# A two-layer graph transformer on one core: the first four blocks of each layer as single tiles

## The chip, the cores and the metric

The kernel runs on one core of a Trainium2 chip. A core has five engines that run their own instruction streams and meet at semaphores: TensorE (PE) for matrix products, VectorE (DVE) and ScalarE (ACT) for element-wise work, GpSimd (POOL), which here mostly starts indirect DMAs, and SyncE (SP), which starts plain ones. Matrix products land in PSUM, everything else lives in SBUF. The metric is the device time of one execution in microseconds, as a median over runs.

## The reference, cut to what matters

There are 2708 tokens with 512 features, and a sparse symmetric adjacency (each row has a few entries beside the diagonal). Two layers with weights of their own do the same thing:

```python
mask = adj.astype(jnp.float32) + jnp.eye(n, dtype=jnp.float32)
q = (h @ Wq.T + bq).reshape(n, N_HEADS, D_K)      # 8 heads of 64
...
scores = jnp.einsum('nhd,mhd->hnm', q, k) / jnp.sqrt(jnp.float32(D_K))
scores = jnp.where(mask[None, :, :] == 0, jnp.float32(-1000000000.0), scores)
attn = jax.nn.softmax(scores, axis=-1)
ctx = jnp.einsum('hnm,mhd->nhd', attn, v).reshape(n, D_MODEL)
h1 = _layer_norm(h + ctx @ Wo.T + bo, ln1_g, ln1_b)
ff = jax.nn.relu(h1 @ W1.T + b1) @ W2.T + b2       # 2048 hidden
h2 = _layer_norm(h1 + ff, ln2_g, ln2_b)
```

Everything is computed in float32.

## The kernel before, in words

**Attention by lists.** The kernel turns the adjacency into lists of neighbours, at most 22 per token, sorts the tokens by the length of their list, and works on 22 tiles of 128 tokens (the last has 20). `CAPS` gives each tile's number of slots: tile 0 has 22, tile 20 has 5. For a slot, POOL gathers one row of keys and values (4 KB) per token. Slots go in chunks of two (`SLOTS`): tile 20 has chunks 20c0, 20c1 and 20c2, the last with one slot. `attend` (from L1436) is a generator; each `next` on it emits one step: the products with the query and their reduction for one chunk (`weights`, L1041 and L1047 on DVE), exp, scaling and summing for the chunk before (`weigh`, L1060 and L1067 on ACT, L1073 and L1080 on DVE), the sums of a tile two steps after its last chunk, and its division by the softmax sum three steps after (`divided`, L1111 on ACT, into `cx`). The step yields its cost, 1 for a chunk of two. After tile 19 and at the end three empty steps of cost 0.2 let these later parts run.

**How attention is woven into the rest.** `advance(more)` adds `more` to a credit and takes steps while the credit is above zero and fewer than two finished contexts wait in `got`. `through(k)` takes steps until block k's contexts are finished. So the code decides the order of the instructions; on PE, ACT and SP it is the order of execution (`manual_schedule`), on POOL it is so until block 0 of layer 0 is done. DVE's stream, and POOL's later, come out of a planner that starts whatever it deems ready first.

**Staging.** In layer 0, keys and values of all tiles are projected beside the building of the lists (`first`), then all queries (`first_queries`), with attention starting beside them. Then the tiles go through the feed-forward in `blocks`: eleven pairs, (20, 19), (18, 17), (7, 9) and so on. For the first block, projection and first normalisation (`attended`) are emitted within the query loop, at its step t = 19, after `through(0)`. For a later block they are emitted while the block before it is in its feed-forward: contexts are transposed at step f = 10 (11 in block 0 of layer 0), projected at the next step, and the normalised rows transposed after step 15 into `hT`, which has one buffer.

**One block's feed-forward** (`feed_forward`) has 16 steps. A step makes 128 of the 2048 hidden features, `pf` (L1351, four products over the block's 256 tokens, in one of three PSUM buffers), puts it through relu (`ft`, L1359, ACT), and three steps later (`LAG`) adds its share to the output sums (L1324), one PSUM accumulator per tile, `a0` and `a1`, with one buffer each. The last three shares come after step 15, tile by tile. DVE reads the accumulators (L1375) and normalises into z. A float32 product shows as two matmul records in the trace: a step of a pair has eight records of `pf` and four of `a`.

**What else runs in it.** In layer 0 each block's z is transposed at steps 5 to 8 of the next block and projected to keys and values of layer 1, which POOL scatters (`keys_values`, `behind`). In layer 1, queries of tiles from `order[16]` on are made late: `blocks[k + AHEAD]` with `AHEAD = 8`, so two per block in blocks 0 to 2, from transposed rows that SP loads. Block 0 of layer 0 also loads the last three pieces of W1 and W2, and layer 1's Wk and Wv, through ACT's queue. The credit per step is `PACE` (0.62 in layer 0, 0.72 in layer 1), and 1.1 up to step 10 and 0.4 after it in block 0 of both layers.

Of the kernel before, what the change touches and what calls it, by code (L numbers as in the profile page):

```python
# [18 lines left out]
P = 128  # L19
# [23 lines left out]
AHEAD = 8  # L43
# [6 lines left out]
PACE = (0.62, 0.72)  # L50
# [422 lines left out]
def by_edges(ctx: ExitStack, tc: tile.TileContext, x, xT, adj, layers, out, good):  # L473
# [125 lines left out]
    def size(g):  # L599
        return min(P, N - g * P)  # L600
# [302 lines left out]
    def first_queries(bq, wq, counts, ranked, listed, pa, tokens, meanwhile):  # L903

        nonlocal at
        made = []

        def written():
            t, qs = made.pop(0)
            if t + 2 < NT:  # L910
                out = q_d[0][t * P : (t + 2) * P, :].rearrange("(two p) c -> p two c", p=P)
                nc.sync.dma_start(out=out, in_=qs)
                return
            for i in range(2):
                r = size(t + i)
                nc.sync.dma_start(out=q_d[0][(t + i) * P : (t + i) * P + r, :], in_=qs[:r, i])

        for t in range(NT):
            r = size(t)
            if t % 2 == 0 and made:  # L920
                written()
            q = project(tokens(t, 1), r, wq, "q", other=t % 2 > 0)
            if t == 0:
                ranked(*counts)
                xrs = [own_rows(g) for g in order[:3]]
            if t % 2 == 0:
                qs = wts.tile([P, 2, DM], F32, tag=f"w2_{5 + t // 2 % 3}", name="qs")
                made.append((t, qs))
            nc.vector.scalar_tensor_tensor(
                qs[:r, t % 2], q[:r], DK**-0.5, bq[:r], ALU.mult, ALU.add  # L930
            )
            plus_rest(qs[:r, t % 2], q, r, DK**-0.5)
            if t == OWN - 1:
                listed(True)
                pa.__exit__(None, None, None)
                at = ctx.enter_context(tc.tile_pool(name="at", bufs=2))
                for g in order[:3]:
                    own[g] = at.tile([P, DM], F32, tag="q", name="q", bufs=QB)
                to = dict(own)
                next(ahead)  # L940
            if t == OWN:
                zTs = [turned_own(g, xr) for g, xr in zip(order, xrs)]
                for g, zT in zip(blocks[0], zTs):
                    own_query(g, zT, to[g], bq, wq)
                    advance(0.5)
            if t == OWN + 1:
                listed(False)
                xr = own_rows(order[3])
            if t == OWN + 4:
                own_query(order[2], zTs[2], to[order[2]], bq, wq)  # L950
                zT = turned_own(order[3], xr)
            meanwhile(t)
            if t == NT - 1:
                g = order[3]
                own[g] = at.tile([P, DM], F32, tag="q", name="q", bufs=QB)
                own_query(g, zT, own[g], bq, wq)
        while made:
            written()
        all_made.append(True)
# [469 lines left out]
    now = Layer(0, layers[0])  # L1429


    blocks = [(20, 19), (18, 17), (7, 9), (6, 10), (5, 11), (0, 16)]
    blocks += [(1, 15), (2, 14), (3, 13), (4, 12), (NT - 1, 8)]
    NB = len(blocks)
    order = [g for block in blocks for g in block]

    def attend(n, got):

        peak = small.tile([P, NT], F32, tag="peak", name="peak", bufs=1)
        nc.vector.memset(peak, 0.0)  # L1440
        loaded = loads(n)
        steps = []
        for g in order:
            cuts = chunks_of(g)
            steps += [(g, s0, c, i, i + 1 == len(cuts)) for i, (_, s0, c) in enumerate(cuts)]
            if g == order[1]:
                steps += [None] * 3
        steps += [None] * 3
        kv = next(loaded)
        yield 0.0  # L1450
        q = asked(n, order[0])
        done = [None] * 3
        for k, step in enumerate(steps):
            if step:
                g, s0, c, i, last = step
                if i == 0:
                    while q is None:
                        q = asked(n, g)
                        if q is None:
                            yield None  # L1460
                    t, q = Tile(g, q), None
                if k > 0:
                    kv = next(loaded)
                t.weights(kv, s0, c)
                if i > 0 and q is None and g != order[-1]:
                    q = asked(n, order[order.index(g) + 1])
                done.append((t, kv, s0, c, last))
            else:
                done.append(None)
            t3, t2, t1 = done[-4:-1]  # L1470
            if t1:
                t1[0].weigh(*t1[1:4])
            if t2 and t2[-1]:
                t2[0].sums(peak)
            if t3 and t3[-1]:
                got[t3[0].g] = t3[0].divided()
            yield c / SLOTS if step else 0.2
        nc.vector.tensor_reduce(flags[:, 4 + n : 5 + n], peak, AX.X, ALU.max)
        nc.vector.tensor_scalar(
            flags[:, 4 + n : 5 + n], flags[:, 4 + n : 5 + n], SAFE, None, ALU.is_le  # L1480
        )
# [3 lines left out]
    def advance(more):  # L1485

        nonlocal credit
        credit = min(credit + more, 1.5)
        while credit > 0 and len(got) < CXB - 1:
            cost = next(ahead, None)  # L1490
            if cost is None:
                break
            credit -= cost
# [44 lines left out]
    behind, pool = None, []  # L1538
    for n in range(NL):
        last = n == NL - 1  # L1540
        nxt = None if last else Layer(n + 1, layers[n + 1])
        if n > 0:
            streamed = now.queries(order[8 : 2 * AHEAD])
            got = {}
            ahead = attend(n, got)
            with tc.manual_schedule(engines={mybir.EngineType.DVE}):
                for _ in range(2):
                    now.query(*pool.pop(0))
                next(ahead)
                next(streamed)  # L1550
                while pool:
                    advance(0.4)
                    now.query(*pool.pop(0))
                for i in range(2 * AHEAD - 10):
                    advance(0.4)
                    next(streamed)
                through(0)
                early[n] = now.attended(blocks[0], got)
                next(early[n])
                for _ in blocks[0]:  # L1560
                    next(early[n])
                finish(streamed)
            now.load_w2(NFC // 2 - 1)
# [6 lines left out]
        for k, block in enumerate(blocks):  # L1570
            more = k + 1 < NB
            asking = iter(())
            if n > 0 and k + AHEAD < NB:
                asking = now.queries(blocks[k + AHEAD])
            for f, zs in enumerate(now.feed_forward(block, hs, hT)):
                if f == NFC:
                    break
                if f in (5, 6, 7, 8) and behind:
                    next(behind)
                if more and f == 10 + (k + n == 0):  # L1580
                    through(k + 1)
                    projecting = now.attended(blocks[k + 1], got)
                    next(projecting)
                if more and f == 11 + (k + n == 0):
                    for hs_next in projecting:
                        advance(0.5 if k else 0.0)
                advance(PACE[n] if k else 1.1 if f < 11 else 0.4)
                if f in (0, 3, 7, 9):
                    next(asking, None)
                if more and f == NFC - 1:  # L1590
# [5 lines left out]
                if n > 0 and (k, f) == (0, 2):  # L1596
                    now.load_second(1, temp)
                if not last:
                    if (k, f) == (0, 10):
                        now.load_next()  # L1600
                        now.kv = [matrix(nxt.w, "Wk", "wk", nc.scalar)]
                    if (k, f) == (0, 13):
                        now.kv.append(matrix(nxt.w, "Wv", "wv", nc.scalar))
                    if (k, f) == (NB - 1, 0):
                        finish(ahead)
                        places.clear()
                        now.wq = matrix(nxt.w, "Wq", "wq")
                    if f == 1 and k in (1, 3):
                        i, name, scale = (1, "bk", 1.0) if k == 1 else (0, "bq", DK**-0.5)
                        turning = turned_row(now.cols[i], name, scale)  # L1610
                        rows_of = now if k == 1 else nxt
                        setattr(rows_of, name, next(turning))
                    if f == 3 and k in (1, 3):
                        finish(turning)
# [19 lines left out]
        else:  # L1634
# [8 lines left out]
            now = nxt  # L1643
# [63 lines left out]
```

## Time and profile before

Three runs took 1942.04 us in the median (1936.44 to 1943.61).

| What | us |
|---|---|
| the profiled execution | 1946.15 |
| its span, first to last instruction | 1944.3 |
| PE busy | 1858.4 |
| DVE busy | 1321.0 |
| ACT busy | 934.7 |
| POOL busy | 809.3 |
| PE idle before transposes of contexts, waiting for ACT (4 times) | 25.5 |
| PE idle before transposes of h, waiting for DVE (4 times) | 10.1 |

The mean granted PE clock is 0.981 of full speed. A line of the timeline gives the start and the length of a run of like instructions in us, the engine, the line of the kernel, the operation, its output and inputs by the program's names, shapes and count, and in brackets the idle time of the engine before it with what ended it. Matmuls overlap in the records, so a run's throughput is read from one start to the next. In the page's slices each digit is the busy share of a fortieth of the span in tenths.

### The profile page before, as it was taken

The numbers are of one execution on the slowest core, as the hardware profiler recorded it, in microseconds if no ns is written. First come the engines' busy times: TensorE is split into PE (matmuls) and PEld (weight loads), VectorE is DVE, ScalarE is ACT, GpSimd is POOL, SyncE is SP. The second block draws the span as 40 slices with busy tenths as digits, with TensorE's granted clock in tenths as the row PEclk, the third lists the DMA queues.
The fourth block names the chain that finished last, engine by engine and source line by source line (L and its number), as shares of the span: only waits on it lengthen the run. The fifth ranks groups of instructions, "written<-read, shape, count | busy, mean of one in ns | idle before, by whom it ended". The sixth has DMA issues, their size and how long they took to land. (4 is left out here: it accounts for less than half of the span.)

```text
span 1944.3 us, 20898 instructions
## 1 busy us (share of the span) xinstructions
PE 1858.4 (96%) x6162; PEld 1096.7 (56%) x6162; DVE 1321.0 (68%) x2172; ACT 934.7 (48%) x3219; POOL 809.3 (42%) x710
## 2 busy tenths in 40 slices
PE   9998968999999999999999997999999999999996
PEld 4443435556656556665665553566666666666663
DVE  5885467768759687695841237696987998877421
ACT  4660236445546655574451113555475767654510
POOL 3113526535536555364410124344555775546101
PEclk9999979999999999999999998999999999999998
DMA  9998848555646656554401478656665766643000
GB/s 322 355 314 299 275 136 302 172 179 184 205 138 201 217 188 197 177 183 154 146 17 65 136 246 325 202 197 204 203 222 168 251 222 220 209 155 125 17 6 14
DMA packets 131486, 366.92 MB, mean 189 GB/s; under 512 B 16668, under 2 KB 37004, under 8 KB 128654
## 3 DMA queue, kind: packets, MB, share of 16 engines
q0 software_dynamic: 69120, 246.35, 38.0%
q1 hardware_dynamic: 53332, 99.66, 14.8%
q10 hardware_dynamic: 8910, 19.48, 2.6%
q8 instruction: 50, 0.82, 0.2%
q14 instruction: 74, 0.61, 0.1%
HBM read 314.62 MB, written 50.83 MB: 188 GB/s over the span
## 5 line engine op out<-in xcount | busy, mean ns | idle before, releaser
L1004 POOL DMA_INDIRECT kv<-kv_d,idx x420 | 547.0, 1302 | 452.2 <-DVE acc L1080 273.5
L1351 PE MATMUL pf<-hT,w 128*128 128x256 f32 (+1 forms) x2816 | 637.2, 373 | 7.2 <-ACT ft L1359 5.2
L1324 PE MATMUL a<-w,ft 128*128 128x512 f32 x1344 | 632.2, 596 | 5.3 <-ACT ft L1359 4.4
L1351 PEld LDWEIGHTS pf<-hT,w 128*128 128x128 f32 x2816 | 521.2, 191 | 186.6 <-issue 106.5
L1359 ACT ACTIVATE ft<-pf,b 128x256 f32<-128x256 f32 (+1 forms) x352 | 160.3, 460 | 458.5 <-PE pf L1351 458.3
L1041 DVE TENSOR_TENSOR kv<-kv,q 128x1024 f32<-128x1024 f32 (+3 forms) x222 | 254.2, 1157 | 169.2 <-DMA kv<-kv_d,idx 131.1
L1324 PEld LDWEIGHTS a<-w,ft 128*128 128x128 f32 x1344 | 253.2, 191 | 198.6 <-issue 171.6
L1067 ACT ACTIVATE kv<-kv,p 128x64 f32<-128x64 f32 x1232 | 311.0, 335 | 5.0
L1047 DVE TENSOR_REDUCE sc<-kv 128x16 f32<-128x1024 f32 (+3 forms) x222 | 253.8, 1153 | 1.5
L1080 DVE TENSOR_TENSOR acc<-acc,kv 128x1024 f32<-128x1024 f32 (+2 forms) x178 | 204.0, 1146 | 18.9 <-ACT kv L1067 17.0
L1156 POOL TENSOR_TENSOR rd<-va,mhalf 128x1 f32<-128x1 f32 (+1 forms) x88 | 90.4, 1028 | 274.6 <-DVE va L1154 273.7
L576 PE MATMUL o<-wo,cT 128*128 128x512 f32 x336 | 151.1, 602 | 0.5 <-ACT cT L1171 0.5
L1073 DVE TENSOR_TENSOR kv<-kv,p 128x512 f32<-128x512 f32 (+1 forms) x178 | 121.4, 682 | 34.6 <-ACT p L1060 34.6
L1060 ACT ACTIVATE p<-sc,minus 128x8 f32<-128x8 f32 x420 | 102.8, 294 | 69.2 <-DVE sc L1047 62.1
L1111 ACT ACTIVATE cx<-acc,su 128x64 f32<-128x64 f32 (+1 forms) x352 | 88.5, 334 | 74.7 <-DVE su L1103 57.6
L576 PEld LDWEIGHTS o<-wo,cT 128*128 128x128 f32 x336 | 64.5, 193 | 83.2 <-issue 72.9
L681 ACT ACTIVATE code<-aj 128x2708 bf16<-128x2708 int32 (+1 forms) x22 | 73.3, 3332 | 49.2 <-POOL aj L677 49.0
L684 DVE MAX8 tops<-code 128x8 f32<-128x247 f32 (+2 forms) x242 | 83.1, 401 | 19.3 <-ACT code L681 19.3
L1160 DVE SCALAR_TENSOR_TENSOR h<-h,rd,ln_b 128x512 f32<-128x512 f32 (+1 forms) x88 | 65.6, 747 | 40.6 <-POOL rd L1156 40.6
L1067 ACT ACTIVATE acc<-kv,p 128x64 f32<-128x64 f32 (+1 forms) x352 | 88.8, 334 | 1.4
L1410 ACT COPY kvs<-v 128x512 f32<-128x512 f32 (+1 forms) x22 | 12.9, 586 | 158.9 <-PE v L576 138.5
L1375 DVE TENSOR_TENSOR h<-a,h 128x512 f32<-128x512 f32 (+1 forms) x44 | 29.9, 679 | 85.2 <-PE a L1339 48.8
(154 smaller groups left out, 1560.2 us busy)
## 6 DMA issues: line engine op xcount, KB each, us to landing
aj<-in_adj SPq DMA_DIRECT2D x21, 1354.0 KB, 8.4
kv_d<-kvs ACTq DMA_DIRECT2D x21, 512.0 KB, 7.4
w<-in_W SPq DMA_DIRECT2D x20, 512.0 KB, 6.5
xg<-in_xT SPq DMA_DIRECT2D x19, 512.0 KB, 8.6
kv<-kv_d,idx POOLq DMA_INDIRECT x420, 5.8
w<-in_W ACTq DMA_DIRECT2D x12, 512.0 KB, 7.2
q_d<-qs SPq DMA_DIRECT2D x22, 256.0 KB, 3.4
zT_d<-zT SPq DMA_DIRECT2D x22, 256.0 KB, 4.3
```

The costliest lines, as they stand in the source:

```text
L576: nc.tensor.matmul(o[:r], xs(c), wm[:, c, :], start=(c == 0), stop=(c == NC - 1))
L1004: nc.gpsimd.indirect_dma_start(out=to, out_offset=None, in_=table[:, :], in_offset=bass.IndirectOffsetOnAxis(ap=s, axis=0), bounds_check=N ...
L1041: nc.vector.tensor_tensor(kv[:r, :c, :DM], kv[:r, :c, :DM], self.q[:r].unsqueeze(1).to_broadcast([r, c, DM]), ALU.mult,)
L1047: nc.vector.tensor_reduce(self.sc[:r, s0 : s0 + c, :], kv[:r, :c, :DM].rearrange("p s (h d) -> p s h d", d=DK), AX.X, ALU.add,)
L1060: nc.scalar.activation(p[:r, s, :], self.sc[:r, s, :], AF.Exp, bias=minus[:r, g, s : s + 1])
L1067: nc.scalar.activation(to[:, i, hd], kv[:r, i, DM + h * DK : DM + (h + 1) * DK], AF.Copy, scale=p[:r, s0 + i, h : h + 1],)
L1073: nc.vector.tensor_tensor(to[:, 0, :].rearrange("p (h d) -> p h d", d=DK), kv[:r, 0, DM:].rearrange("p (h d) -> p h d", d=DK), p[:r, s0, : ...
L1080: nc.vector.tensor_tensor(self.acc[:r, :c, :], self.acc[:r, :c, :], kv[:r, :c, DM:], ALU.add)
L1156: nc.gpsimd.tensor_tensor(rd[:r], va[:r], mhalf[:r], ALU.pow)
L1324: nc.tensor.matmul(a[:r], fts[f][:, c0 : c0 + r], self.w2[f // 2][:, f % 2, :], start=(f == 0), stop=(f == NFC - 1),)
L1351: nc.tensor.matmul(pf[:, :w], self.w1[f // 2][:, c, f % 2 * P : f % 2 * P + P], hT[:, c, :w], start=(c == 0), stop=(c == NC - 1),)
L1359: nc.scalar.activation(ft[:, :w], pf[:, :w], AF.Relu, bias=self.b1[:, f : f + 1])
```

## The change

Tiles 20, 19, 18 and 17 become blocks of one tile each; the other nine blocks stay as they are, so a layer has thirteen blocks where it had eleven. What depends on the width of a block follows:

- `through(0)` and the projection of block 0 concern tile 20 alone; the three empty steps of attention after tile 19 are left out.
- A single tile's block transposes the next block's contexts at step 8 and projects them at step 9; for pairs these are steps 10 and 11 everywhere.
- A single tile's block advances attention by 0.45 a step, and by nothing beside the projection; pairs keep `PACE`, scaled by their tokens over 256 (1 for a full pair).
- Late queries of layer 1 are taken in order, as many as the block has tiles.
- Loads for layer 1 (`load_next`, Wk, Wv) move from steps 10 and 13 of block 0 to steps 6 and 9.

```diff
-                for g, zT in zip(blocks[0], zTs):
+                for g, zT in zip(order[:2], zTs):
...
-    blocks = [(20, 19), (18, 17), (7, 9), (6, 10), (5, 11), (0, 16)]
+    blocks = [(20,), (19,), (18,), (17,), (7, 9), (6, 10), (5, 11), (0, 16)]
...
-            if g == order[1]:
-                steps += [None] * 3
...
+            late = order[2 * AHEAD :]
...
-            if n > 0 and k + AHEAD < NB:
-                asking = now.queries(blocks[k + AHEAD])
+            wide = sum(size(g) for g in block) / (2 * P)
+            if n > 0 and late:
+                asking = now.queries(late[: len(block)])
+                late = late[len(block) :]
...
-                    next(behind)
-                if more and f == 10 + (k + n == 0):
+                    next(behind, None)
+                turn = 10 - 2 * (len(block) == 1)
+                if more and f == turn:
...
-                if more and f == 11 + (k + n == 0):
+                if more and f == turn + 1:
                     for hs_next in projecting:
-                        advance(0.5 if k else 0.0)
-                advance(PACE[n] if k else 1.1 if f < 11 else 0.4)
+                        advance(0.5 if len(block) > 1 else 0.0)
+                advance(PACE[n] * wide if len(block) > 1 else 0.45)
...
-                    if (k, f) == (0, 10):
+                    if (k, f) == (0, 6):
...
-                    if (k, f) == (0, 13):
+                    if (k, f) == (0, 9):
```

## The prediction

> **What bounds the kernel now.** I read the page's busy times first, then its slices, then the timeline of TensorE (PE) where the slices drop. PE is the bound: it is busy 96% of the span, VectorE (DVE) 68%, ScalarE (ACT) 48%.
>
> ```profile
> PE 1858.4 (96%) x6162; PEld 1096.7 (56%) x6162; DVE 1321.0 (68%) x2172; ACT 934.7 (48%) x3219; POOL 809.3 (42%) x710
> ...
> PE   9998968999999999999999997999999999999996
> ...
> PEclk9999979999999999999999998999999999999998
> ```
>
> Each digit is 48.6 us. PE drops in slice 6 (243 to 292 us) and slice 25 (1215 to 1264 us), and the granted clock drops with it: these are the entries into the feed-forward (FF) of the two layers, which the change touches. The timeline shows what is waited for there. First layer 0, columns: start, length, engine and line, operation, idle time before it and its releaser.
>
> ```profile
> 248.34 0.60 PE L1166 MATMUL tp<-ident,cx 128*128 128x128 f32 x4
> 263.15 1.91 PE L1166 MATMUL tp<-ident,cx 128*128 128x128 f32 x4 [14.21 <-ACT cx L1111]
> ...
> 285.24 1.11 PE L1166 MATMUL tp<-ident,h 128*128 128x128 f32 x4 [3.66 <-DVE h L1160]
> 286.81 9.03 PE L1351 MATMUL pf<-hT,w 128*128 128x256 f32 x32 [0.46 <-ACT hT L1171]
> ```
>
> Tile 20's context is transposed at 248.34; PE then sits 14.21 us for tile 19's, since both belong to block 0. Layer 1 repeats it:
>
> ```profile
> 1203.84 0.60 PE L1166 MATMUL tp<-ident,cx 128*128 128x128 f32 x4
> 1211.87 1.91 PE L1166 MATMUL tp<-ident,cx 128*128 128x128 f32 x4 [7.43 <-ACT cx L1111]
> ...
> 1232.91 7.17 PE L1351 MATMUL pf<-hT,w 128*128 128x256 f32 x32 [1.05 <-ACT hT L1171]
> ```
>
> Undisturbed work, for prices: a pair's FF step, and 128-column matmuls with a fresh weight load each.
>
> ```profile
> 601.05 1.04 PE L1166 MATMUL tp<-ident,h 128*128 128x128 f32 x8
> 601.93 5.32 PE L1324 MATMUL a<-w,ft 128*128 128x512 f32 x12
> ...
> 615.70 1.89 PE L1351 MATMUL pf<-hT,w 128*128 128x256 f32 x8
> 617.43 1.88 PE L1324 MATMUL a<-w,ft 128*128 128x512 f32 x4
> 619.15 1.89 PE L1351 MATMUL pf<-hT,w 128*128 128x256 f32 x8
> ```
>
> Start to start counts here, since lengths overlap. A pair's step is 619.15 - 615.70 = 3.45 us; eight 128-column matmul records take 601.93 - 601.05 = 0.88 us, 0.11 each; the 512-column ones 1.72 / 4 = 0.43.
>
> **Two rules of the Trainium skill.** "TensorE: Matmul & The Clock Gate", section on LDWEIGHTS, prices a weight load by its columns, 128 / 1.2 = 107 ns, so a matmul over 128 columns cannot run faster than its weights arrive. The trace agrees (0.11 us), and I use 0.11: the halved matmul costs just over half of the 256-column one (1.73 / 8 = 0.216), no cliff. Part 1 of the same page says that the clock halves after about 3.4 us of idleness. Here the v matmuls at 403.00, after only 2.05 us idle, took 5.40 us against 3.60 at 390.48, so shorter gaps cost too; the forecast goes by the trace.
>
> **The change, part by part.**
>
> *Matmul shape.* A single's step is 8 x 0.11 + 2 x 0.43 = 1.746 us (0.111 and 0.429 before rounding), 27.9 us for 16 steps; two singles cost 55.9 where a pair costs 16 x 3.45 = 55.1. Four singles stand for two pairs in each layer: +1.4 us a layer.
>
> *Entry of layer 0.* `through(0)` now needs tile 20 alone. But the three empty steps after tile 19 are gone, so the credits of the query loop (0.5 + 0.5 + 5 x 1.0 + 0.6) now also put 18c0 and 18c1 (tile 18's first two chunks) ahead of block 0's projection in program order on ACT and POOL, where in before they came behind it. On POOL, tile 20's row gather (246.68 in before) then stands behind the gather of 17c1, which waits for the buffer of 18c0: the DMA let DVE start 18c0 at 253.19; product and reduction take 2.5, exp and copies 2.5, so the buffer is free near 259.5. Two gathers of 1.3 and the row gather end near 264; landing takes 5 (5.8 median): h of tile 20 can be added at about 269, its normalisation takes 5.5 (275.4 to 280.9 in before), and DVE owes up to 2 us of other work: 276. Transpose and copy 1.6: FF starts near 278, not 286.8. PE then still owes tile 19's projection and transposes.
>
> *Blocks 0 to 3 of layer 0.* Before: 286.81 to 449.55 for blocks 0 and 1, 162.7 us. Their work at full rate is 110.3 (steps) + 4 projections of 3.43 + 10 transposes of 0.44 + 2 key-value tiles of 6.87 + one turned row 0.9 = 143.1; 19.6 us are idle time (5.2 for ACT in block 0's steps, 3.14, 0.85, 2.05) and half clock. After: 111.7 + 5 x 3.43 + 13 x 0.44 + 3 x 6.87 + 1.8 = 157, ending at 435 plus new stalls. Before reaches equal work at 449.55 + 7.3 (keys of tile 18) + 0.9 = 457.8. Gain 22.8 us, less the stalls.
>
> *Entry of layer 1.* Tile 20's cx was done at 1196.6, so projection follows its transpose at once: 1204.3 + 1.3 (copy) + 3.43 = 1209; two queries to 1216, under which the normalisation (3.9 us after the projection's end in before) hides; FF near 1217.8, not 1232.9. Owed: one projection and two transposes, 4.3. Gain 10.8, less 1.4 for shape.
>
> *New stalls.* PE's slack halves while DVE and ACT work per tile stays.
> - Accumulator `a0` (one buffer, L1324). In a pair, the first tile's sum is taken up by DVE 4.4 us (typical; 1.6 to 7.2) after its last matmul, while PE has 2.6 us of the other tile and 6.9 of the next block's first four groups. In a single, PE is back in `a0` after 4 x 0.888 = 3.55. The read ends at 4.4 + 0.7 = 5.1: 1.6 us, at three boundaries per layer: 9.6 us. Bounds: 0 (DVE at once) and 3.5 each.
> - Relu (L1359) behind attention copies on ACT. In pairs it starts up to 4.8 us late (6.7 at worst) without a stall, because three PSUM buffers give 3 x 1.72 + 2 x 1.73 = 8.6 us; a single gives 3 x 0.86 + 2 x 0.888 = 4.35, of which 0.4 is the relu itself. The pace rises from 0.62 or 0.72 in 3.45 us to 0.45 in 1.746, one chunk in 3.9 us, against 2.5 us of ACT and on average 3.9 us of DVE (860 us of attention groups over 222 chunks). So DVE keeps pace only without other work, and it owes 5 us of h and 3.3 of z per tile. The gate of two waiting contexts gives it rest. I take 1 us per single, 8 in all; bounds 0 and 4 each.
> - Turned z for keys (layer 0): z is normalised about 6 us after the add, so 10.4 after the block; the transpose comes at 7.9 + 1.6: 0.9 x 3 = 3 us.
> - h of the next tile: 10.5 us from the projection's end to its transpose, against 8.5 typical in before: nothing, up to 2 each.
> - Block 0 of layer 0: cold clock as in before 2 us; the loads of w1 and w2 (3 MB) and of Wk and Wv (2 MB, moved from steps 10 and 13 to 6 and 9 on ACT's queue) now fall into 28 us of steps and 4 of projection beside 9 chunks of 1 MB. 14 MB at the 400 GB/s seen near 220 us take 35 us: 3 us, bounds 0 and 7. The small loads on SP ahead of it move with it; the rows are due a block later: nothing.
> - Half clock after a 2 us stall, 1.7 us each, twice: 3.
>
> Late queries are the same six tiles, one per single and then a pair, 3.43 us each wherever they stand; attention asks for them later: nothing. Pace and step numbers of full pairs are unchanged (except one step in layer 0's block 0).
>
> *Sum.* Gains 22.8 + 10.8 = 33.6; losses 1.4 (layer 1; layer 0's shape is in its 157) + 9.6 + 8 + 3 + 5 + 3 = 30. Net 3.6 us off the profiled execution's 1946.15 (span 1944.3, 1.9 around it): 1942.5. The median of the runs is 4.1 lower, so 1938.4, call it 1938.
>
> **The rivals.** *Faster:* the planner orders DVE so that the sum of a single is read at once and relu stays in its slack; then only 1.4 + 2 + 6 are lost and 24 us stay: 1918. For it: DVE is idle 27% of the time between 287 and 450 (119.7 of 163 us busy in the table by stage), and it ran ahead by a whole tile at 1196 to 1211. Against it: the lag at `a0` is about 4 us in most pairs. *Slower:* relu in singles. One mechanism: a DVE backlog of h, z and chunks reaches ACT, whose in-order queue holds relu behind exp, and PE stops; before's block 0, paced at one chunk in 3.1 us, had relus 15 us late and 5.2 us idle. Break-even is at 4 us lost per single (32 / 8), and my sum has 3.6; at 6.5 each the loss is 52 and the time 1942 + 20 = 1962. *Given back:* what layer 0 wins (22.8 less its stalls, 4.8 + 4 + 3 + 5 + 1.5: 4.5) could be lost again where tile 0's 22 slots bind (6.56 us idle between 650 and 700). Then layer 1's balance, 10.8 - 11.7, decides: 1943. Against it: attention is gated by PE's own use of contexts, so this wait should move along with PE.
>
> **How the numbers follow.** Half a percent, 9.7 us, is about what a measurement of this kernel can tell from no change. The balanced case (no change; own range 1929 to 1953) gets 0.36, the one given back 0.05, the faster rival 0.27, the slower 0.32. 0.02 of the balanced case lies above half a percent: faster 0.27, same 0.39, slower 0.34. The range takes both rivals in: 1914 to 1966.
>
> **What would show it.** In the trace of after: FF near 278 and 1218; `a` waits for DVE at the single boundaries of 1 to 2 us; `pf` waits for ft up to 1 us per single; a single's step of 1.75 us where undisturbed; pair (7,9)'s first step near 453 in layer 0 (449.55 in before, with a key-value tile less done) and some 4 us ahead of before's 1375.5 in layer 1. A single's step well above 1.75 without waits, or an FF start still at 286, would make it wrong.

## The result, and the profile after

The changed kernel takes 1957.18 us in the median of 8 runs (1949.68 to 1963.89), the kernel before in the same comparison 1942.82 (1936.38 to 1945.73). The ratio is 1.0070, with a 95 per cent interval of 1.0052 to 1.0087: slower by more than the half percent that counts as a change here. The forecast was 1938.

The page of the kernel after, busy times and slices (one digit is 48.9 us):

```profile
PE 1864.7 (95%) x6674; PEld 1117.4 (57%) x6674; DVE 1322.4 (68%) x2172; ACT 948.4 (48%) x3283; POOL 799.7 (41%) x710
...
PE   9999977999999999999999998989999999999996
...
PEclk9999988999999999999999999999999999999998
```

Of the 11.8 us by which the span grew (1944.3 to 1956.1), PE is busy 6.3 more and idle 5.5 more. The dip in the slice of layer 1's entry is shallower (8 where it was 7, and the clock digit there is back at 9). The one in layer 0 has become slices 6 and 7 (245 to 342 us), and the granted clock is down in both. PE's waits, first after, then before; columns us in total, times, longest:

```profile
PE tp L1166 <- DVE h L1160: 21.7, 7, 6.8
PE pf L1351 <- ACT hT L1171: 8.7, 6, 3.4
PE a L1324 <- DVE h L1375: 8.3, 3, 4.0
...
PE tp L1166 <- ACT cx L1111: 3.8, 1, 3.8
```

```profile
PE pf L1351 <- ACT ft L1359: 5.2, 3, 2.9
...
PE pf L1351 <- ACT hT L1171: 2.1, 3, 1.1
...
PE a L1324 <- DVE va L1154: 0.9, 1, 0.9
```

The 25.5 us of waiting for contexts shrank to 3.8; that is what single tiles at the front can do. But the waits for h (the name covers a row before and after the feed-forward) doubled from 10.1, the wait of `pf` for hT rose from 2.1 to 8.7, and the sum's accumulator, which cost before 0.9, takes 8.3. Relu's 5.2 us in front of `pf` are gone. The timeline of PE in layer 0 shows where:

```profile
270.13 1.11 PE L1166 MATMUL tp<-ident,h 128*128 128x128 f32 x4 [4.76 <-DVE h L1160]
271.75 5.87 PE L1351 MATMUL pf<-hT,w 128*128 128x128 f32 x32 [0.51 <-ACT hT L1171]
...
278.31 1.05 PE L1351 MATMUL pf<-hT,w 128*128 128x128 f32 x8
279.20 1.02 PE L1324 MATMUL a<-w,ft 128*128 128x512 f32 x2
280.07 1.05 PE L1351 MATMUL pf<-hT,w 128*128 128x128 f32 x8
...
311.62 1.12 PE L1166 MATMUL tp<-ident,h 128*128 128x128 f32 x4 [6.80 <-DVE h L1160]
...
325.05 2.07 PE L1324 MATMUL a<-w,ft 128*128 128x512 f32 x2 [3.98 <-DVE h L1375]
...
363.37 0.66 PE L1166 MATMUL tp<-ident,h 128*128 128x128 f32 x4 [1.41 <-DVE h L1160]
...
408.29 2.94 PE L1324 MATMUL a<-w,ft 128*128 128x512 f32 x4 [2.12 <-ACT ft L1359]
```

The FF of layer 0 starts at 271.75, against 286.81 before, and a single's step takes 280.07 - 278.31 = 1.76 us. Then the three boundaries between singles have waits of up to 6.80 us. The four blocks end at the first `pf` of pair (7, 9), at 460.90; before reaches the same work near 457.8 by the prediction's account. So 15 us of head start are gone, and 3 more.

The table by stage gives the rest. Columns: stretch, its length, PE busy, weight loads, DVE, ACT, POOL busy (with counts), granted clock, DMA share, GB/s; first after, then before, each for the singles (or the same work) of layer 0 and of layer 1:

```profile
271.70:460.90 189.20, 168.40 (x796) 111.19 (x796) 125.92 (x184) 95.69 (x364) 84.57 (x72) 0.94 0.58 191
1225.60:1385.80 160.20, 149.44 (x752) 99.19 (x752) 123.53 (x173) 98.63 (x387) 70.07 (x59) 1.00 0.62 202
```

```profile
286.80:457.80 171.00, 159.78 (x532) 100.08 (x533) 127.69 (x179) 93.09 (x355) 87.21 (x70) 0.96 0.63 211
1232.90:1375.50 142.60, 141.69 (x480) 88.26 (x481) 117.96 (x160) 90.39 (x349) 70.89 (x58) 1.00 0.67 226
```

Layer 0: 189.2 us for 157 of work (the prediction's price), 32 lost. Before loses about 20 of its 171: its stretch holds 151 of work, since the projection and two transposes of tile 19 lie ahead of it there and pairs cost 1.4 less. About 11 of the 32 are clock (an estimate, 6 per cent of 189.2), the others are waits of PE: 8.8 for h, 4.0 for `a0`, 3.5 for relu, 3.4 for hT, 1.2 for the copy of a turned context. Layer 1 loses no clock: its 160.2 us hold 148.3 of work (before's 142.6, and 5.7 for what is owed and for the shape), and 10.8 of the difference are named waits. It starts at 1225.61, against 1232.91 in a stream that was 8.7 us ahead (the last block of layer 0 starts at 1088.6 before and at 1097.3 after), and ends 10.3 behind before: of layer 1's own, 1.6.

### The profile page after: what moved, and what is told of

It reads as the page before. It is cut to its first block, busy times and chain, and to the rows that moved or that the text cites. A ratio compares the mean times of both kernels' runs of the same rounds, so it can differ in the third digit from the quotient of the medians.

```text
span 1956.1 us, 22006 instructions
## 1 busy us (share of the span) xinstructions
PE 1864.7 (95%) x6674; PEld 1117.4 (57%) x6674; DVE 1322.4 (68%) x2172; ACT 948.4 (48%) x3283; POOL 799.7 (41%) x710
## 5 line engine op out<-in xcount | busy, mean ns | idle before, releaser
L1351 PEld LDWEIGHTS pf<-hT,w 128*128 128x128 f32 x3328 | 557.6, 193 | 199.7 <-issue 130.9
L1351 PE MATMUL pf<-hT,w 128*128 128x256 f32 (+2 forms) x3328 | 652.0, 343 | 8.7 <-ACT hT L1171 8.7
L1324 PE MATMUL a<-w,ft 128*128 128x512 f32 x1344 | 645.0, 599 | 13.8 <-DVE h L1375 8.3
L1359 ACT ACTIVATE ft<-pf,b 128x256 f32<-128x256 f32 (+2 forms) x416 | 175.8, 428 | 489.8 <-PE pf L1351 488.2
L1324 PEld LDWEIGHTS a<-w,ft 128*128 128x128 f32 x1344 | 246.1, 192 | 178.5 <-issue 144.7
L1156 POOL TENSOR_TENSOR rd<-va,mhalf 128x1 f32<-128x1 f32 (+1 forms) x88 | 88.0, 1000 | 264.4 <-DVE va L1154 263.4
L576 PEld LDWEIGHTS o<-wo,cT 128*128 128x128 f32 x336 | 63.9, 192 | 89.2 <-issue 68.8
L1417 POOL DMA_INDIRECT kv_d<-kvs,ident_i x22 | 23.2, 1052 | 163.9 <-ACT kvs L1410 95.7
```

The lines of the kernel that those rows point to most:

```text
L576: nc.tensor.matmul(o[:r], xs(c), wm[:, c, :], start=(c == 0), stop=(c == NC - 1))
L1324: nc.tensor.matmul(a[:r], fts[f][:, c0 : c0 + r], self.w2[f // 2][:, f % 2, :], start=(f == 0), stop=(f == NFC - 1),)
L1351: nc.tensor.matmul(pf[:, :w], self.w1[f // 2][:, c, f % 2 * P : f % 2 * P + P], hT[:, c, :w], start=(c == 0), stop=(c == NC - 1),)
L1359: nc.scalar.activation(ft[:, :w], pf[:, :w], AF.Relu, bias=self.b1[:, f : f + 1])
```

## The experiments

Diffs are against the changed kernel where nothing else is said. All ratios are to the kernel before, with 95 per cent intervals.

**Which layer.** One layer with four singles, the other with before's pairs (and their empty steps, pace, turn and loads). This is l0_only; in l1_only the two lists of `starts` are exchanged:

```diff
-    blocks = [(20,), (19,), (18,), (17,), (7, 9), (6, 10), (5, 11), (0, 16)]
+    starts = [(20,), (19,), (18,), (17,)], [(20, 19), (18, 17)]
+    tail = [(7, 9), (6, 10), (5, 11), (0, 16)]
...
+        blocks = starts[n] + tail
```

> Singles in layer 0 alone; layer 1 as in the kernel before. If the loss arises in layer 0 (its four singles took 189 us where their work is 157, and pair (2,14) later stood 4.2 us longer), this kernel is 8 to 9 us slower than before: about 1951. If layer 1 carries the loss, it is within 3 us of before: 1940 to 1946.

> Singles in layer 1 alone; layer 0 as in the kernel before. By the trace of the changed kernel layer 1's singles gain 11.7 us at the entry and lose 11.9 in their blocks, with 1.4 for the matmul shape: 1 to 3 us slower than before, about 1945. If the two layers' losses are alike, it is 6 to 7 us slower, about 1949.

Measured 1.0061 (1.0049 to 1.0073) and 1.0006 (0.9996 to 1.0015). The two add up to the whole, and layer 0 carries it. In layer 1 the earlier start and the stalls of the singles cancel.

**Which single.** Two singles and then the pair (18, 17), in both layers (two, the first diff); and the other way round, a pair first and then two singles, in layer 0 alone (late_two, the second; layer 1 with pairs, the rest as before):

```diff
-    blocks = [(20,), (19,), (18,), (17,), (7, 9), (6, 10), (5, 11), (0, 16)]
+    blocks = [(20,), (19,), (18, 17), (7, 9), (6, 10), (5, 11), (0, 16)]
```

```diff
-    blocks = [(20,), (19,), (18,), (17,), (7, 9), (6, 10), (5, 11), (0, 16)]
+    starts = [(20, 19), (18,), (17,)], [(20, 19), (18, 17)]
+    tail = [(7, 9), (6, 10), (5, 11), (0, 16)]
...
+        blocks = starts[n] + tail
```

> Only tiles 20 and 19 as singles, then the pair (18,17). The early entry stays. If the stalls at the boundaries between singles make the loss, two of the three boundaries of each layer go with their waits (layer 0: 1.4, 1.4, 2.1, 0.5; layer 1: 2.0 and 3.2) and half of the shape's cost (2 us), while the 6.8 and 4.0 us after block 0 stay: 1942 to 1947. If the entry itself, with block 0 as a single, makes it, it stays at 1953 to 1958.

> Layer 0 with the pair (20,19) first and then singles 18 and 17; everything else as in the kernel before (layer 1 too). No early entry, so this is the bare price of two singles. If a single costs stalls at its boundaries even where DVE is not behind (8 us in blocks 2 and 3 of the changed kernel, and 1.4 to 2 for the shape), it is 8 to 12 us slower than before: 1951 to 1955. If those stalls were the tail of block 0's backlog, it is within 4 us of before.

Measured 1.0005 (0.9995 to 1.0016) for the first two singles, 1.0045 (1.0031 to 1.0060) for two singles that come with no early entry. The timelines of PE, of late_two and then of the same work in before, show what these cost:

```profile
365.98 1.83 PE L1324 MATMUL a<-w,ft 128*128 128x512 f32 x2 [2.27 <-DVE h L1375]
...
375.74 0.66 PE L1166 MATMUL tp<-ident,h 128*128 128x128 f32 x4 [2.15 <-DVE h L1160]
...
415.28 1.98 PE L1324 MATMUL a<-w,ft 128*128 128x512 f32 x4 [0.79 <-ACT ft L1359]
...
465.18 8.86 PE L1351 MATMUL pf<-hT,w 128*128 128x256 f32 x32 [3.36 <-ACT hT L1171]
```

```profile
373.98 1.12 PE L1324 MATMUL a<-w,ft 128*128 128x512 f32 x2 [0.85 <-DVE va L1154]
...
403.00 5.40 PE L576 MATMUL v<-wv,zT 128*128 128x512 f32 x8 [2.05 <-DVE kvs L1407]
```

The two singles wait 9 us in all (the wait at 375.74 is for a finished row, z, on its way to keys and values; a small one is left out), where the pair of before waits 2.9. Behind them the next pair's first 32 records of `pf` take 8.86 us, against about 7.1 undisturbed. The last wait is that of a pair behind a single: eight copies of hT (2.14 us of ACT) lie behind only the single's last three shares, 6 x 0.43 = 2.6 us of PE. It has the same 3.35 or 3.36 us in after, alt_acc, q_early and here.

**Which wait.** The sum: singles take the two accumulators in turn (alt_acc).

```diff
-            accs = [ps_a.tile([P, DM], F32, tag=f"a{i}", name=f"a{i}") for i in range(len(block))]
+            first = len(block) == 1 and order.index(block[0]) % 2
+            accs = [
+                ps_a.tile([P, DM], F32, tag=f"a{i + first}", name=f"a{i + first}")
+                for i in range(len(block))
+            ]
```

> The changed kernel, with singles using accumulators a0 and a1 in turn, so that a single never waits for the sum of the one before it. If the one accumulator costs what its waits show (8.3 us in three waits, and up to 3 us of half clock behind them), the time falls to 1946 to 1949. If DVE's lag only shows up in the next wait (relu, h or hT), it stays at 1953 to 1957.

Measured 1.0056 (1.0040 to 1.0072). The wait for `a0` is gone, and in block 1 of layer 0 the transpose of z, a few us later, waits 3.66 us instead. By the intervals it can't be told from the change.

The row h: the next tile's contexts are transposed and projected two steps earlier (turn6).

```diff
-                turn = 10 - 2 * (len(block) == 1)
+                turn = 10 - 4 * (len(block) == 1)
```

> The changed kernel, with the next tile's contexts turned at step 6 and projected at step 7 of a single, instead of 8 and 9. It gives h 3.5 us more before its transpose. If h's wait (8.8 us in layer 0, 6.8 of it after block 0) and the half clock behind it are the price of too short a notice, they shrink by 3.5 us per boundary: 1950 to 1953. If DVE puts h behind its attention work whenever the projection comes, nothing is won: 1955 to 1959.

Measured 1.0054 (1.0036 to 1.0072), not told apart from the change. PE in turn6:

```profile
306.35 0.65 PE L1166 MATMUL tp<-ident,h 128*128 128x128 f32 x4 [1.12 <-DVE h L1160]
...
320.92 2.07 PE L1324 MATMUL a<-w,ft 128*128 128x512 f32 x2 [12.20 <-ACT ft L1359]
```

The wait for h falls from 6.80 to 1.12, and one of 12.20 us for relu comes in the next block. So the wait for h can be taken away and the time stays; the reading, not tested further, is that work which was ahead of h is then ahead of something else. Both edits on top of the two-singles kernel (two_alt6) did nothing that shows either:

> Two singles, then pairs; the singles use the two accumulators in turn and turn the next contexts at step 6. If the waits left in the kernel with two singles (h 6.9, sums 3.6 in layer 0, and half clock) go with these two edits, it is faster than before: 1932 to 1937. If they only move, it stays at 1942 to 1945.

Measured 1.0007 (0.9991 to 1.0022), against 1.0005 without them.

**What is not it.** The loads of W for layer 1, put back to steps 10 and 13 (loads_late):

```diff
-                    if (k, f) == (0, 6):
+                    if (k, f) == (0, 10):
...
-                    if (k, f) == (0, 9):
+                    if (k, f) == (0, 13):
```

> The changed kernel, with the loads for layer 1 back at steps 10 and 13 of block 0. If the 2 MB of Wk and Wv beside the gathers hold up block 0 (3 us in the prediction, up to 7), the time falls to 1950 to 1954. If they do not, it stays at 1956 to 1958.

Measured 1.0071 (1.0044 to 1.0099): no gain is seen, though an interval this wide leaves room for some 5 us either way. In its trace the wait for h after block 0 falls to 2.75 us and the sum's next wait grows from 3.98 to 7.25: again a wait that moved.

In block 0 DVE stands 5.63 us for a gathered query. Asking for the next query at a tile's first chunk instead of its second, in the changed kernel (q_early), in two (two_q) and in the kernel before (before_q):

```diff
-            if i > 0 and q is None and g != order[-1]:
+            if q is None and g != order[-1]:
```

> The changed kernel, with the query of the next tile asked for at the first chunk of a tile instead of the second. In layer 0's block 0 DVE stood 5.6 us before tile 7's first chunk, waiting for that query's gather, and h of tile 19 and the sums of tile 17 stood behind it. If this block of DVE makes the 6.8 us at h (and relu 10 us late beside it), they shrink and 4 to 8 us are won: 1949 to 1953. If DVE would have been late anyway, 1955 to 1959.

> Two singles, then pairs, with the early query. The kernel with two singles stood with before (1.0005); it still has the wait for h after block 0 (6.9 us), the sum's (3.6) and half clock. If the early query takes these away, it beats before: 1934 to 1939. If not, 1941 to 1945.

> The kernel before, with the query asked for at the first chunk, as the counterpart of the same edit on the changed kernel. If the query's gather holds DVE up only where block 0 is a single, no change: 1940 to 1945. If it holds up block 0 of before as well (its PE stood 5.2 us for relu there), 1937 to 1940.

Measured 1.0044 (1.0029 to 1.0060), 0.9977 (0.9962 to 0.9992) and 0.9975 (0.9963 to 0.9987): about a quarter of a percent in each of the three (in the changed kernel the intervals with and without it overlap). It is a gain that the kernel before has as well, so it does not explain the loss. The wait for h in q_early is still 5.85 us.

**Attention's pace.** First everywhere in singles (pace30):

```diff
-                advance(PACE[n] * wide if len(block) > 1 else 0.45)
+                advance(PACE[n] * wide if len(block) > 1 else 0.3)
```

> The changed kernel, with attention advanced by 0.30 a step in singles instead of 0.45, so that DVE and ACT have a third less attention ahead of h, sums and relu there; the attention left out is made up in the pairs. If a backlog of attention on DVE and ACT makes the stalls of the singles, most of layer 0's waits in the blocks (about 18 us) go, less what the pairs give back: 1945 to 1951. If the waits come from the short chain itself, 1955 to 1959.

Measured 1.0430 (1.0399 to 1.0462), far outside both expectations. In block 0 it does what was hoped: from its first `pf` to that of block 1 are 36.2 us instead of 45.6. But attention has then fallen behind for good: the next three pairs take 81.2 to 94.4 us in layer 0, where they take 72.5 to 87.8 in after, and layer 1's four singles 188.6 instead of 160.2.

DVE's timeline in after shows why block 0 is so long. The projection of tile 19 began at 290.61 and took 3.70, so its product was there at 294.3:

```profile
296.14 1.23 DVE L1041 TENSOR_TENSOR kv<-kv,q 128x1024 f32<-128x1024 f32 x1 [5.63 <-DMA q<-q_d,ident_i]
297.28 0.20 DVE L1092 TENSOR_REDUCE peak<-sc 128x1 f32<-128x56 f32 x1
297.40 1.22 DVE L1047 TENSOR_REDUCE sc<-kv 128x16 f32<-128x1024 f32 x1
...
305.01 1.23 DVE L1080 TENSOR_TENSOR acc<-acc,kv 128x1024 f32<-128x1024 f32 x1
306.15 0.68 DVE L1293 TENSOR_TENSOR h<-o,xb 128x512 f32<-128x512 f32 x1
...
310.82 0.75 DVE L1160 SCALAR_TENSOR_TENSOR h<-h,rd,ln_b 128x512 f32<-128x512 f32 x1
```

The first step to h (L1293) starts 11.9 us after its product. It adds the tile's own row, `xb`, and POOL's timeline and the row's landing tell how the 11.9 us divide:

```profile
291.65 1.00 POOL L1004 DMA_INDIRECT xb<-in_x,ident_i  x1 [0.30 <-issue]
...
DMA to landing us min/median/max: 3.7/7.2/9.3
```

The row of tile 19 (the first of two issued there) is the slowest of the four between 235 and 330 us: issued at 291.65, it landed 9.3 us later, at about 300.9. From 280 to 300 us the DMA engines had no room (their share reads 1.03, at 378 and then 407 GB/s). So 6.6 of the 11.9 us passed before h could be added at all. Only the other 5.2 are DVE's order: the planner put attention operations (and four small ones of a later stage, left out above) ahead of it. The query for which DVE stood 5.63 us came through the same full DMA engines. Less attention beside block 0 should shorten both delays, so the pace was lowered in that one block only: with two singles (two_b0slow) and with four (after_b0slow), the first diff, and, as a control, in the kernel before (before_b0slow, the second diff, against before), where 0.62 all through block 0 replaces 1.1 and then 0.4.

```diff
-                advance(PACE[n] * wide if len(block) > 1 else 0.45)
+                advance(PACE[n] * wide if len(block) > 1 else 0.45 if k + n else 0.3)
```

```diff
-                advance(PACE[n] if k else 1.1 if f < 11 else 0.4)
+                advance(PACE[n] if k or n == 0 else 1.1 if f < 11 else 0.4)
```

> Blocks (20,), (19,), (18, 17) in both layers, with attention paced at 0.3 instead of 0.45 per step in block 0 of layer 0 alone. If the early entry of layer 0 is lost because attention operations stand ahead of h in VectorE's order in block 0, the wait of h's transposition for the second tile falls from 6.9 to 2 us or less and the time is 1935 to 1939. If the supply of attention is the limit, what block 0 leaves undone is made up for in the blocks behind it: 1943 to 1950.

> The changed kernel with attention paced at 0.3 instead of 0.45 per step in block 0 of layer 0 alone. The same edit was worth 0.51 per cent with two single tiles. If the loss of the change has two parts that do not touch each other (the order of VectorE in block 0, and the bare price of the third and fourth single), the ratio to the kernel before is 1.001 to 1.003. If the slower pace only moves attention into the two further singles, which have less cover, it stays at 1.005 to 1.008.

> The kernel before with 0.62 per step all through block 0 of layer 0, instead of 1.1 up to step 10 and 0.4 behind it. If a slower block 0 is a gain of its own that has nothing to do with single tiles: 0.994 to 0.997. If it pays only where a single tile has moved the start of the feed-forward ahead: 0.999 or above.

Measured 0.9954 (0.9937 to 0.9971), 1.0024 (1.0014 to 1.0034) and 1.0074 (1.0056 to 1.0092). Four kernels differ in just two things and make a square:

| First blocks, both layers | 0.45 in block 0 of layer 0 | 0.30 there |
|---|---|---|
| two singles, then a pair | 1.0005 | 0.9954 |
| four singles | 1.0070 | 1.0024 |

Each column differs by 0.65 to 0.70 per cent, each row by 0.46 to 0.51: the two costs hardly touch each other. PE in two_b0slow, from the wait for h of tile 19 on:

```profile
303.81 0.65 PE L1166 MATMUL tp<-ident,h 128*128 128x128 f32 x4 [1.58 <-DVE h L1160]
...
306.88 3.73 PE L1351 MATMUL pf<-hT,w 128*128 128x128 f32 x32
...
316.60 2.07 PE L1324 MATMUL a<-w,ft 128*128 128x512 f32 x2 [5.99 <-DVE h L1375]
```

Block 0 takes 36.1 us instead of 46.0 in two, and the wait for h falls from 6.93 to 1.58. DVE adds h right behind one product and one reduction, at 298.29. From h's product to its row's landing are 5.1 us (6.8 in two), and from there to DVE's addition 1.5 (5.1 in two): most of what is won is in DVE's order, a part in the DMA engines. Part of it comes back at once, as a wait of 5.99 for the sum. By the ratios 0.5 per cent stay, or some 10 us.

The control shows that a slow block 0 is no gain in itself. In before_b0slow that block is 2 us shorter, but pair (7, 9) then starts at 459.2 instead of 449.5, and it is h again:

```profile
447.01 1.12 PE L1166 MATMUL tp<-ident,h 128*128 128x128 f32 x4 [9.73 <-DVE h L1160]
```

Its product was there by 423.5, and DVE added it at 439.01, behind attention operations of which one stood 3.68 us for its gather.

**The best of it.** two_b0slow with alternating accumulators and the early query, edits as above:

> The same, with the two single tiles taking different accumulators and the next tile's query asked for at the first chunk. If the three costs are apart from each other: 1929 to 1934. If a cost taken away comes back as another wait, as it did with the later turn: 1938 to 1944.

Measured 0.9943 (0.9920 to 0.9965), 1931.61 us: faster than both kernels, but not told apart from two_b0slow (1934.69). The sum's wait of 5.99 is gone from block 1, and in its place the transpose of z waits 7.12 at 323.18. Whether the three gains add up is not decided: the median lies in the range expected if they do; the sum of their single gains would be about 0.991, just outside the interval, and the early query's alone, 0.993, lies in it.

## Why the prediction was wrong

*Matmul shape: right.* A step is 1.755 us (1.746 forecast). Four singles for two pairs cost PE's pure work next to nothing. That the weight load sets this price is not shown: 128, 256 and 512 columns cost 0.11, 0.216 and 0.43 us, in proportion to the columns.

*Entry of layer 0: right in kind, better in size.* FF starts at 271.75, not 278. The row gather went out at 260.17 behind the two gathers it was put behind, and landed at 265.62; normalisation took 4.4 us, not 5.5 and 2 owed.

*Blocks 0 to 3 of layer 0: this step failed.* The forecast had 18.3 us of losses in the 157 of work, the trace has 32:

| Loss in layer 0's singles, us | forecast | trace of after |
|---|---|---|
| h of the next tile | 0 | 8.8 |
| half clock, in block 0 and after stalls | 3.5 | 11 |
| hT behind a single | 0 | 3.4 |
| copy of a turned context | 0 | 1.2 |
| the sum's accumulator | 4.8 | 4.0 |
| relu | 4 | 3.5 |
| turned z | 3 | 0 |
| loads beside block 0 | 3 | none seen |

The term with the largest error is "h of the next tile: nothing, up to 2 each". It is 6.80, 1.41 and 0.55, and the longest is followed by half clock, whose term is too small by nearly as much. The working took the age of h (10.5 us from projection to transpose, 8.5 typical) from blocks that run at their pace, and set it against PE's time. It asked neither when the gathered row lands while loads and gathers fill the DMA engines (6.6 us of the 11.9 in block 0) nor where DVE's order, which the planner makes, puts h among attention (5.2). Block 0 took 45.6 us for about 32 of work, so most of the head start was spent when block 1 began, at 317.33.

The square shows attention in block 0 to be a cause: slowing it there returns half a percent. By which way, DVE's order, the DMA engines or ACT, is not separated, since fewer attention steps relieve all three; and turn6 and loads_late show that taking the wait for h away does not by itself give the time back.

The square also tells where the forecast did not fail. By its own terms (an estimate: two of three accumulator boundaries, two singles' relu and the shape in both layers, turned z in layer 0) the third and fourth single cost 13.6 us; the columns differ by 12.6 to 13.6. That the sum fits is in part luck, since relu was taken too high and hT left out. With two singles the same terms give about 0.991, and 1.0005 was measured. So the error, 0.9 per cent, lies in what the two kernels share, the first blocks and what follows from them. The slower pace gives back about half of it, and the rest is open.

*The other stalls.* The accumulator: 8.3 in both layers against 9.6, right in sum, but unevenly (3.98, 1.12, 3.16). Relu: nothing in layer 1, against 4. Turned z: none in after, but 3.66 in alt_acc, where the accumulator no longer waits first. hT behind a single: 0.61, 2.02 and 1.75 in layer 1 as well. Loads: loads_late shows no gain, but its interval does not exclude the 3 us.

*Half clock.* Before has about 7 us of it in the same work. Part 1 of "TensorE: Matmul & The Clock Gate" in the Trainium skill speaks of about 3.4 us of idleness before the clock falls; here 2.12 us of idle time at 408.29 are followed by four records of `a` in 2.94 us, where an undisturbed run of four in a pair takes 1.88, so the measurement decides. In layer 0 the waits of the singles cost about 1.5 times themselves (32 us for 21).

*Entry of layer 1: right.* Against a stream that was 8.7 us behind, FF started 16.0 us earlier (15.1 forecast), and its singles lost 11.9 (10.3 forecast). l1_only agrees with the balance: 1.0006.

*Behind the singles: not forecast.* The feed-forward of pair (1, 15) in layer 0 took 85.3 us, 4.2 more than before: at its end PE waited 4.76 for h of the next pair, and in DVE that row waited 2.82 for `rd` (L1156), which POOL made behind gathers. This is one profiled execution, and no run here tests it.

Of the rivals, the slower one gave the right side and nearly the right time (1962), but named relu. What happened is a kin of it: attention ahead of the block's own work, met by h instead of by relu. turn6 shows how close they lie, since 12.20 us of relu appear when h is moved out of the way. The rival of a gain given back at tile 0's slots is not seen: the feed-forward of (5, 11), in which PE waits for them, took 87.8 us after and 89.2 before.

## What to carry to other kernels

Halving a block halves the time in which the other engines' work for the next block must be done, while that work stays; sum the boundary waits (row, sum, transposed row) for the new cover before counting on an earlier start. Where a planner or a written order decides what stands ahead of the row that PE waits for, look up that place in the trace, and look up when the row's own transfer landed. Of what was tried here, the early start paid only with two singles and with what is woven in beside it slowed in that block alone (0.9954; with four singles 1.0024, and 1.0430 when slowed in all of them). And try each wait's removal alone: here three of them, the sum's, h's by an earlier turn and h's by later loads, came back under another name.

## What was not expected of the hardware

The clock: waits of 2 to 7 us in the singles of layer 0 cost 11 us of clock beside 21 of waiting, and the same kind of waits in layer 1 (up to 3.16 us) none: the granted clock there is 1.00. No run here settles why.

One execution's profile is a weak witness for a few microseconds. The stream of layer 0 in l1_only is that of before, yet its last block started at 1080.5 in one profile and at 1088.6 in the other. So the sums of waits above, and the table by terms, say where time stands in one execution; what a change costs is taken from the ratios.
